# Counting the edge matrix of a graph network in steps of two edge tiles by 28 destinations

## The chip, the cores and the metric

The kernel runs on one core of one Trainium2 chip. The time is that of one execution on the device in microseconds; several runs were made, and their median counts.

## The reference

A graph of N = 6250 nodes with 128 features and E = 100000 edges. Edges are sorted by their destination `dst`, which is drawn as 6250 times the square of a uniform number, so low destinations have many more edges than high ones; `src` and the edge type (8 relations) are uniform. Two graph networks follow one another, each with a residual and a layer norm:

```python
def _rgcn_conv(x, src, dst, etype, bases_l, comp_l, root_l, bias_l):
    weight = jnp.einsum('rb,bio->rio', comp_l, bases_l)
    h = jnp.einsum('ni,rio->nro', x, weight)
    msg = h[src, etype]
    seg = dst * R + etype
    cnt = segment_sum(ones, seg, num_segments=N * R)
    norm = 1.0 / jnp.maximum(cnt[seg], 1.0)
    agg = segment_sum(msg * norm[:, None], dst, num_segments=N)
    return agg + x @ root_l + bias_l
# three such layers, batch norm and relu between them; then
#   x = layernorm(x + rgcn(x))
h = x @ W_in + b_in                         # 128 -> 64
deg = segment_sum(ones(E), src, N)
edge_weight = rsqrt(deg)[src] * rsqrt(deg)[dst]    # 0 where deg is 0
acc = cur = h
for _ in range(3):
    cur = segment_sum(cur[dst] * edge_weight[:, None], src, N)
    acc = acc + cur
x = layernorm(x + (acc / 4) @ W_out + b_out)
```

The three passes at the end multiply `cur` by one and the same matrix, whose element (src, dst) is the number of edges from src to dst. That matrix is what the change is about.

## The kernel before

Nodes are put into 49 blocks of 128 (NBLK = 49, NP = 6272), edges into 782 tiles of 128.

**Layers (window_sums).** For each tile, `one_sum` (lines 1046 to 1051) issues an indirect DMA on POOL that gathers 128 rows of `h_d` into a buffer `gt` (27 buffers), and a matmul on PE (L1051) sums them by destination with a one-hot `o`, which DVE makes for eight tiles at once (L1040, L1042). After each group of two tiles DVE adds the sum in PSUM to `agg` (L1630). Each layer gathers for 100 tiles of rows of x in `first_sums`, beside the matmuls that make h (L956), and for 590 tiles of rows of h in its window. The edges of the destinations with most edges are summed in another way, by `dense_sums`: seven chunks, each with a load of packed counts, preparation on DVE and ACT (L1326 to L1345) in single buffers, and 42 matmuls (L1352); its end are L1369 to L1383.

**Side work.** The layers' loop takes turns with other work, a generator `side_work`: first `hot_counts` (packed counts for dense_sums) and `degrees` (L1403 to L1415) in layer 0, then `counts`, which makes the edge matrix. `take_turns` spreads N_SIDE side turns over TURNS tiles. While dense_sums runs, its turns take the place of the side turns. The order in which the instructions stand on each engine is set when the program is built, and each engine works through its own in that order.

**The edge matrix.** Counts are packed into 32-bit words: a word has six fields (FLD = 6) of four bits, each for another block of src. There are NSL = 9 slices, so that one destination has S = 9 x 128 = 1152 words. `counts` goes through the edges in steps of TS = 4 tiles. A step adds to the words of one block of 128 destinations; a block whose edges reach over several steps is carried on, and there are NST = 245 steps. In each step:

- DVE makes `dst_hot` for four tiles (L1560, 128 x 512), the one-hot of the destination within the block.
- For each tile (a unit) DVE makes `row` (L1564): 1152 columns, in which one word holds 1 shifted to the field of this edge's src.
- PE multiplies dst_hot (weights, 128 columns) by row (moving, in pieces of 512, 512 and 128 columns) into three PSUM banks (L1577).
- `leave` adds each piece to what is carried, `had` times `keep` (L1535, three operations), and SP issues a DMA of `had` to `a_d` in DRAM (L1546), whose condition, read into registers for eight steps at a time, is true only where a block is done: 49 times of 245. The DMA writes 576 KB in pieces of 512 bytes.

Rows have four buffers (rp), had three (ac), dst_hot two (cp), and PSUM pool ps_w has five banks, which dense_sums takes all of.

**The tail.** Three passes, each over nine slices of src and seven chunks of seven blocks of destinations. SP loads a chunk `packed` (128 destinations by 7 x 128 words, 3584 bytes in a run; ten buffers), DVE splits it into two halves of fields (`u`, L1831 and L1832), and PE takes one field of one block at a time as weights and `three`, which holds cur in three bfloat16 parts and a one, as the moving side (L1837): 7203 matmuls.

Of the kernel before, what the change touches and what calls it, by code (L numbers as in the profile page):

```python
# [17 lines left out]
P = 128  # L18
# [501 lines left out]
def sorted_path(  # L520
# [34 lines left out]

    nc = tc.nc
# [48 lines left out]
    NG4 = Q * J // TS  # L605
    NST = NG4 + NBLK
# [6 lines left out]
    assert T1 + AND <= HT and P1 == 2 and W == 4 * P1 * P and 15 * NS1 <= NST * TS  # L613
    assert D == P and N * R <= 1 << 16 and R == 8 and H == 64
    assert 96 < Q <= P and N + P <= PAD and NBLK % CH == 0 and J == 2 * TS and NST <= 256
# [498 lines left out]
    ac = tc.alloc_tile_pool(name="ac", bufs=3)  # L1114
# [4 lines left out]
    a_d = dram.tile([NSL, P, NBLK, P], I32, name="a_d")  # L1119
    iota_c = kp.tile([P, S], mybir.dt.int16, name="iota_c")  # L1120
    nc.gpsimd.iota(iota_c, pattern=[[1, S]], base=0, channel_multiplier=0)
# [4 lines left out]
    nc.gpsimd.iota(iota_q, pattern=[[0, 1]], base=0, channel_multiplier=2,  # L1126
                   allow_small_or_imprecise_dtypes=True)

    e_src, e_rel, rel_s, e_val = (kp.tile([P, NST, TS], F32, name=f"e_tab{k}") for k in range(4))
# [10 lines left out]
    def hot_counts():  # L1140
# [130 lines left out]
        had = ac.tile([P, S], I32, name="had")  # L1271
        nc.vector.memset(had[:, :SR], 0)
        made, sums, at = {}, {}, {}
        for i in range(NS1 + 2):
            if i < NS1:
                hot = cp.tile([P, TS, P], BF16, name="dst_hot")
                nc.vector.tensor_tensor(hot[:, :P1, :], iota_f[:, None, :].to_broadcast([P, P1, P]),
                                        e_lo[:, i, :, None].to_broadcast([P, P1, P]), op=OP.is_equal)
                rows = []
                for j in range(P1):  # L1280
                    row = rp.tile([P, S], BF16, name="row")
                    nc.vector.tensor_scalar(row[:, :SR], iota_c[:, :SR], e_col[:, i, j : j + 1],
                                            e_v[:, i, j : j + 1], op0=OP.is_equal, op1=OP.mult)
                    rows.append(row)
                made[i] = hot, rows
            s = i - 1
            if 0 <= s < NS1:
                hot, rows = made.pop(s)
                sums[s] = ps_w.tile([P, 512], F32, name="pw")
                for j in range(P1):  # L1290
                    nc.tensor.matmul(sums[s][:, :SR], hot[:, j, :], rows[j][:, :SR], start=(j == 0),
                                     stop=(j == P1 - 1))
            s = i - 2
            if s >= 0:
                now = ac.tile([P, S], I32, name="had")
                nc.vector.scalar_tensor_tensor(now[:, :SR], had[:, :SR], keep[:, s : s + 1],
# [8 lines left out]
                nc.sync.dma_start(c1_d[:, bass.ds(at[0, s], 1), :], now[:, None, :SR], cond=(at[1, s] == 1))  # L1305
# [121 lines left out]
    def counts():  # L1427

        B = NBLK
        edge = kp.tile([P, B], F32, name="edge")  # L1430
        nc.vector.tensor_scalar(edge, iota_f[:, :B], float(P), None, op0=OP.mult)
        d_in = dst_f[:, 1 : W + 1]
        p_t = [ps_w.tile([P, 512], F32, name="pw")[:B, :1] for _ in range(2)]
        for h in range(2):
            below = [cp.tile([Q, B], F32, name=f"below{k}") for k in range(2)]
            nc.vector.tensor_scalar(below[0], edge[:Q, :], d_in[:, h * 512 + 511 : h * 512 + 512], None,
                                    op0=OP.is_gt)
            nc.vector.tensor_scalar(below[1], edge[:Q, :], float(P), d_in[:, h * 512 : h * 512 + 1],
                                    op0=OP.add, op1=OP.is_gt)
            for k in range(2):  # L1440
                nc.tensor.matmul(p_t[k], below[k], ones[:Q, :1], start=(h == 0), stop=(h == 1))
        col = kp.tile([B, 8], F32, name="col")
        t0, n, incl, s0, delta, pos, top = (col[:, i : i + 1] for i in range(7))
        nc.vector.tensor_copy(t0, p_t[0])
        nc.vector.tensor_tensor(n, p_t[1], t0, op=OP.subtract)
# [3 lines left out]
        p_i = ps_w.tile([P, 512], F32, name="pw")[:B, :1]  # L1449
        nc.tensor.matmul(p_i, upto, n, start=True, stop=True)  # L1450
        nc.vector.tensor_copy(incl, p_i)
        nc.vector.tensor_sub(s0, incl, n)
        nc.vector.tensor_sub(delta, t0, s0)
        nc.vector.tensor_scalar_add(top, incl, -1.0)
        yield

        fld = kp.tile([B, 2], F32, name="fld")
        nc.vector.tensor_scalar(fld[:, 0:1], iota_p[:B, :], float(NSL), None, op0=OP.is_ge)
        for j in range(2, FLD):
            nc.vector.scalar_tensor_tensor(fld[:, 0:1], iota_p[:B, :], float(j * NSL), fld[:, 0:1],  # L1460
                                           op0=OP.is_ge, op1=OP.add)
        nc.vector.scalar_tensor_tensor(fld[:, 1:2], fld[:, 0:1], -float(NSL), iota_p[:B, :],
                                       op0=OP.mult, op1=OP.add)
        FULL = NBLK - (FLD - 1) * NSL
        nc.vector.tensor_scalar(pos, fld[:, 1:2], -float(FULL), 0.0, op0=OP.add, op1=OP.max)
        nc.vector.tensor_sub(pos, fld[:, 0:1], pos)
        nc.vector.scalar_tensor_tensor(pos, fld[:, 1:2], float(FLD), pos, op0=OP.mult, op1=OP.add)

        past, within, start_, ends = (flat(e_val)[:B, i * NST : (i + 1) * NST] for i in range(4))
        nc.vector.tensor_scalar(past, iota_s[:B, :], incl, None, op0=OP.is_ge)  # L1470
        nc.vector.tensor_scalar(within, iota_s[:B, :], s0, None, op0=OP.is_ge)
        nc.vector.tensor_sub(within, within, past)
        nc.vector.tensor_scalar(start_, iota_s[:B, :], s0, None, op0=OP.is_equal)
        nc.vector.tensor_scalar(ends, iota_s[:B, :], top, None, op0=OP.is_equal)
# [3 lines left out]
        p_b = ps_w.tile([P, 512], F32, name="pw")  # L1478
        nc.tensor.matmul(p_b[:, :NST], ones[:B, :], past, start=True, stop=True)
        nc.vector.tensor_scalar(step_b, p_b[:, :NST], float(P), None, op0=OP.mult)  # L1480
        p_g = ps_w.tile([P, 512], F32, name="pw")
        delta_b = kp.tile([B, P], F32, name="delta_b")
        nc.vector.tensor_copy(delta_b, delta.to_broadcast([B, P]))
        nc.tensor.matmul(p_g[:, :NST], delta_b, within, start=True, stop=True)
        nc.vector.tensor_add(step_g, p_g[:, :NST], iota_s)
        p_k = ps_w.tile([P, 512], F32, name="pw")
        nc.tensor.matmul(p_k[:, :NST], ones[:B, :], start_, start=True, stop=True)
        nc.vector.tensor_scalar(keep, p_k[:, :NST], -1.0, 1.0, op0=OP.mult, op1=OP.add)
        step_i = kp.tile([1, 2, NST], I32, name="step_i")
        for k, of in enumerate((pos, ones[:B, :1])):  # L1490
            p_e = ps_w.tile([P, 512], F32, name="pw")
            nc.tensor.matmul(p_e[:1, :NST], of, ends, start=True, stop=True)
            nc.vector.tensor_copy(step_i[:, k, :], p_e[:1, :NST])
        yield

        sel = [flat(rel_s)[:Q, h * NST : (h + 1) * NST] for h in range(2)]
        for h in range(2):
# [3 lines left out]
        for to, of in ((e_key, key_f), (e_rel, d_in)):  # L1501
            for j in range(TS):
                pe = ps_w.tile([P, 512], F32, name="pw")
                for h in range(2):
                    c = h * 512 + j * P
                    nc.tensor.matmul(pe[:, :NST], of[:, c : c + P], sel[h], start=(h == 0), stop=(h == 1))
                nc.vector.tensor_copy(to[:, :, j], pe[:, :NST])
                yield
        nc.vector.tensor_scalar(e_key, e_key, 3, None, op0=OP.logical_shift_right)
        nc.vector.tensor_copy(e_src, e_key)  # L1510
        nc.vector.tensor_tensor(rel_s, e_rel, step_b[:, :, None].to_broadcast([P, NST, TS]),
                                op=OP.subtract)
        over = e_rel
        nc.vector.memset(e_val, 1.0)
        for j in range(1, FLD):
            nc.vector.tensor_scalar(over, e_src, float(j * S), 15.0, op0=OP.is_ge, op1=OP.mult)
            nc.vector.scalar_tensor_tensor(e_val, over, 1.0, e_val, op0=OP.add, op1=OP.mult)
        e_fld = over
        nc.vector.tensor_scalar(e_fld, e_src, float(S), None, op0=OP.is_ge)
        for j in range(2, FLD):  # L1520
            nc.vector.scalar_tensor_tensor(e_fld, e_src, float(j * S), e_fld, op0=OP.is_ge, op1=OP.add)
        nc.vector.scalar_tensor_tensor(e_src, e_fld, -float(S), e_src, op0=OP.mult, op1=OP.add)
        yield

        pieces = [(1024, S - 1024), (0, 512), (512, 512)]
        had = ac.tile([P, S], I32, name="had")
# [4 lines left out]
        def leave():  # L1531

            s, k, p, had, now = left.pop(0)
            c, w = pieces[k]
            nc.vector.scalar_tensor_tensor(now[:, c : c + w], had[:, c : c + w], keep[:, s : s + 1],  # L1535
# [386 lines left out]
```

## Time and profile before

| what | value |
|---|---|
| median of 3 runs | 3674.02 us (3672.62 to 3679.8) |
| profiled execution | 4294.16 us |
| its span | 4292.4 us |
| mean granted clock of TensorE | 0.72 |
| PE busy | 2957.9 us (69%) |
| DVE busy | 2451.4 us (57%) |
| POOL busy | 2114.4 us (49%) |

The profiled execution is 17% longer than the median of the runs; all durations from the trace belong to it. PE is the engine of matmuls, PEld its loading of weights (beside PE), DVE the vector engine, ACT the scalar one, POOL the one that issues the gathers, SP the one that issues the other DMAs. A line of a group of instructions gives: line, engine, operation, output <- inputs, partitions x elements and type of output and input, count | busy us, mean ns of one | idle time just before them, and what ended it. A line of waits gives the engine, what waits, what it waited for: us in total, number of times, longest us. "Issue" is time in which an engine waited for nothing that the profile shows, "remote" a wait whose end no engine of this core explains. A line of windows gives the stretch and its length in us, busy time (with the number of instructions) of PE, PEld, DVE, ACT and POOL, the granted clock, and the DMA engines' busy share and GB/s.

### The profile page before, as it was taken

Reading aid. Unit: us, or ns where it says so; the run is one execution under the profiler, and the core shown is the slowest. Engines: PE = TensorE matmul, PEld = TensorE weight load, DVE = VectorE, ACT = ScalarE, POOL = GpSimd, SP = SyncE. Lnnn points to the kernel's source line nnn. Section 1 sums busy time; section 2 is a strip of 40 time slices with the busy share of each in tenths; the row PEclk is TensorE's granted clock in tenths of the full one; section 3 lists DMA queues with packets and bytes.
Section 4 is the critical chain, followed back from the end, with each engine's and each line's share of the span. In section 5 each row is a group of like instructions: output and inputs, shape, how many; then the busy total and the mean of one; then the engine's idle time right before and its main releaser. Section 6 shows DMA issues by size and latency. Waiting matters only on the chain.

```text
span 4292.4 us, 51372 instructions
## 1 busy us (share of the span) xinstructions
PE 2957.9 (69%) x17520; PEld 2063.9 (48%) x17520; DVE 2451.4 (57%) x6315; ACT 322.6 (8%) x600; POOL 2114.4 (49%) x2083
## 2 busy tenths in 40 slices
PE   6745545667649576666666586766666756999998
PEld 3444434443334343334343334433333435999997
DVE  7557756752651376667526613766666435755555
ACT  2400000000005000000000041000000101000000
POOL 5566766564533665666664346655555653000000
PEclk8855555676669666667766687666666766999999
DMA  5511111131127111112231263222222312454542
GB/s 183 182 44 42 50 49 59 37 76 51 40 71 275 49 45 50 55 57 59 62 80 46 78 238 113 59 60 62 60 68 59 91 50 83 139 155 138 151 128 81
DMA packets 274421, 373.10 MB, mean 87 GB/s; under 512 B 86718, under 2 KB 197726, under 8 KB 274148
## 3 DMA queue, kind: packets, MB, share of 16 engines
q1 hardware_dynamic: 199464, 230.31, 16.9%
q0 software_dynamic: 66240, 135.79, 11.2%
q10 hardware_dynamic: 8444, 3.61, 0.3%
q8 instruction: 140, 2.29, 0.2%
q14 instruction: 133, 1.09, 0.1%
HBM read 250.74 MB, written 243.64 MB: 115 GB/s over the span
## 4 chain that ended last, share of the span: by engine, by line
PE 47%; DVE 25%; another core or an unknown queue 14%; issue 11%; DMA 1%; DVEq 1%; POOL 0%; ACTq 0%; ACT 0%; SPq 0%; POOLq 0%
PE pw L1837 13%; PE ps L1051 11%; PE pw L1577 8%; PE pw L956 6%; DVE row L1564 6%; DVE had L1535 5%; PE pw L1352 3%; DVE agg L1630 2%; DVE o L1040 2%; DVE dst_hot L1560 1%; DVE lo_hot L1403 1%; PE pw L1379 1%; PE pw L969 1%; DVE blk_hot L1406 1%
## 5 line engine op out<-in xcount | busy, mean ns | idle before, releaser
L1048 POOL DMA_INDIRECT gt<-h_d,gidx x1770 | 1796.1, 1015 | 1123.8 <-PE ps L1051 589.3
L1577 PE MATMUL pw<-row,dst_hot 128*128 128x128 bf16 (+1 forms) x2940 | 906.2, 439 | 645.2 <-issue 261.8
L1051 PEld LDWEIGHTS ps<-o,gt 128*128 128x128 f32 x4140 | 790.5, 273 | 366.3 <-issue 164.2
L1564 DVE TENSOR_SCALAR row<-iota_c,e_tab,e_tab 128x1152 bf16<-128x1152 int16 x980 | 566.1, 586 | 677.0 <-remote 385.2
L1051 PE MATMUL ps<-o,gt 128*128 128x48 f32 (+1 forms) x4140 | 785.5, 349 | 199.0 <-issue 71.2
L1577 PEld LDWEIGHTS <-dst_hot 128*128 128x128 bf16 x2940 | 353.2, 132 | 1075.0 <-issue 1011.7
L1837 PE MATMUL pw<-three,u 128*128 128x193 bf16 x7203 | 615.0, 248 | 13.8 <-DVE three L1764 10.1
L1837 PEld LDWEIGHTS <-u 128*128 128x128 fp8e3 x7203 | 601.7, 98 | 21.3 <-DVE three L1764 10.2
L1535 DVE SCALAR_TENSOR_TENSOR had<-had,keep,pw 128x128 int32<-128x128 int32 x735 | 444.8, 606 | 1.0 <-PE pw L1577 1.0
L956 PE MATMUL pw<-w,xT 128*128 128x512 f32 x588 | 295.0, 638 | 69.6 <-issue 40.0
L1048 POOL DMA_INDIRECT gt<-x_d,xidx x200 | 195.0, 975 | 268.4 <-PE ps L1051 122.7
L1831 DVE TENSOR_SCALAR u<-packed 128x896 int32<-128x896 int32 x189 | 117.8, 623 | 194.2 <-PE pw L1837 194.1
L1352 PE MATMUL pw<-x,u 128*128 128x385 bf16 x735 | 190.5, 388 | 49.4 <-issue 38.7
L1403 DVE TENSOR_TENSOR lo_hot<-iota_f,e_tab 128x512 bf16<-128x512 f32 x196 | 134.4, 686 | 140.7 <-remote 84.5
L956 PEld LDWEIGHTS pw<-w,xT 128*128 128x128 f32 x588 | 109.9, 202 | 174.0 <-issue 130.0
L1630 DVE TENSOR_TENSOR agg<-agg,ps 128x48 f32 x885 | 174.6, 197 | 31.6 <-PE ps L1051 20.3
L957 ACT COPY hs<-pw 128x512 f32<-128x512 f32 x294 | 171.1, 585 | 252.1 <-remote 119.1
L1415 PE MATMUL pd<-blk_hot,lo_hot 128*128 128x49 bf16 x782 | 62.8, 218 | 183.4 <-DVE blk_hot L1406 74.3
L1040 DVE TENSOR_TENSOR o<-iota_f,lo 128x384 f32<-128x384 f32 x222 | 121.9, 550 | 114.3 <-remote 70.3
L1352 PEld LDWEIGHTS <-u 128*128 128x128 fp8e3 x882 | 95.1, 112 | 157.5 <-issue 114.0
L1560 DVE TENSOR_TENSOR dst_hot<-iota_f,e_tab 128x512 bf16<-128x512 f32 x245 | 167.5, 684 | 0.0
L1415 PEld LDWEIGHTS <-lo_hot 128*128 128x128 bf16 x782 | 63.6, 130 | 207.1 <-DVE lo_hot L1403 132.7
(398 smaller groups left out, 1886.8 us busy)
## 6 DMA issues: line engine op xcount, KB each, us to landing
a_d<-had SPq DMA_DIRECT2D x245, 576.0 KB
packed<-a_d SPq DMA_DIRECT2D x189, 448.0 KB
h_d<-hs SPq DMA_DIRECT2D x147, 512.0 KB
gt<-h_d,gidx POOLq DMA_INDIRECT x1770
c_d<-had SPq DMA_DIRECT2D x62, 196.0 KB
packed<-c_d SPq DMA_DIRECT2D x21, 448.0 KB
x_d<-xc SPq DMA_DIRECT2D x24, 256.0 KB
xc<-in_x_dram SPq DMA_DIRECT2D x19, 256.0 KB
```

Of the source, the lines that this page charges most:

```text
L956: nc.tensor.matmul(ph, xT[:, b * P : (b + 1) * P], w[:, c : c + 512], start=True, stop=True)
L1040: nc.vector.tensor_tensor(o[:, :n, :width], iota_f[:, None, :width].to_broadcast([P, n, width]), column[:, t : t + n, None].to_broadcast([ ...
L1048: nc.gpsimd.indirect_dma_start(out=gt, out_offset=None, in_=table[:, :], in_offset=bass.IndirectOffsetOnAxis(ap=at[:, t : t + 1], axis=0))
L1051: nc.tensor.matmul(pa, gt, o, start=first_, stop=last)
L1352: nc.tensor.matmul(sums[d][:, :C3D], us[d % 2][:, i, :, d // 2], x3[:, i, :], start=(c == 0 and i == 0), stop=(c * CH + i == NBLK - 1))
L1403: nc.vector.tensor_tensor(hot[:, :n, :], iota_f[:, None, :].to_broadcast([P, n, P]), src_lo[:, t0 : t0 + n, None].to_broadcast([P, n, P]), ...
L1535: nc.vector.scalar_tensor_tensor(now[:, c : c + w], had[:, c : c + w], keep[:, s : s + 1], p[:, :w], op0=OP.mult, op1=OP.add)
L1560: nc.vector.tensor_tensor(hots[s], iota_f[:, None, :].to_broadcast([P, TS, P]), rel_s[:, s, :, None].to_broadcast([P, TS, P]), op=OP.is_equal)
L1564: nc.vector.tensor_scalar(rows[i], iota_c, e_src[:, s, j : j + 1], e_val[:, s, j : j + 1], op0=OP.is_equal, op1=OP.mult)
L1577: nc.tensor.matmul(p[:, :w], hots[s][:, j, :], row[:, c : c + w], start=(j == 0), stop=(j == TS - 1))
L1630: nc.vector.tensor_add(to, to, pa)
L1837: nc.tensor.matmul(out_of(f), bytes_[f % 2][:, d, :, f // 2], cur[:, order[c0 + d], :], start=(c0 + d == 0 and f % 2 == 0), stop=(c0 + d = ...
```

## The change

The matrix is counted and stored in another form.

- A step is two tiles (TU = 2) by 28 destinations (DB = 28); NP / DB = 224 blocks, NST = 616 steps. The number of units rises from 980 to 1232.
- The two sides of the count matmul are exchanged. `row` now has 252 columns, one for each of 28 destinations x 9, where the nine are what src / 128 leaves when the field is taken from it; its value is the field's shift, and its two halves of 126 columns (HB) are the weights. The one-hot is that of src's low seven bits (`dst_hot` by name still, made for four units at once) and is moving, 128 columns. A unit takes two matmuls rather than three, into one PSUM bank for each step.
- `had` is one operation of 126 x 256 for each step. The conditional DMA is issued for each of 616 steps, is true for 224, and writes 252 runs of 512 bytes.
- had has five buffers rather than three; iota_c, row and had are 392 elements wide rather than 1152.
- The tables that give each step its edges are made for two tiles a step, in four parts rather than two, and N_SIDE goes from 1263 to 1516 with TURNS unchanged.
- The matrix in DRAM is stored by destination: for each, nine runs of 128 words, one per slice of src. The tail reads a chunk of five or six blocks (each ninth) with runs of 512 bytes: 243 chunks rather than 189, with the same 7203 matmuls.

```diff
     TS = 4
-    NG4 = Q * J // TS
-    NST = NG4 + NBLK
+    TU = 2
+    DB = 28
+    NDB = NP // DB
+    HB = DB * NSL // 2
+    NST = Q * J // TU + NDB
...
-    ac = tc.alloc_tile_pool(name="ac", bufs=3)
+    ac = tc.alloc_tile_pool(name="ac", bufs=5)
...
-    a_d = dram.tile([NSL, P, NBLK, P], I32, name="a_d")
+    a_d = dram.tile([NDB, 2 * HB, P], I32, name="a_d")
...
-            s, k, p, had, now = left.pop(0)
-            c, w = pieces[k]
-            nc.vector.scalar_tensor_tensor(now[:, c : c + w], had[:, c : c + w], keep[:, s : s + 1],
-                                           p[:, :w], op0=OP.mult, op1=OP.add)
-            if k < len(pieces) - 1:
-                return
+            s, p, had, now = left.pop(0)
+            nc.vector.scalar_tensor_tensor(now[:HB, : 2 * P], had[:HB, : 2 * P], keep[:HB, s : s + 1],
+                                           p[:HB, : 2 * P], op0=OP.mult, op1=OP.add)
...
             nc.sync.dma_start(
-                a_d[:, :, bass.ds(at[0, s], 1), :].rearrange("s p d c -> p s (d c)"),
-                now.rearrange("p (s c) -> p s c", c=P), cond=(at[1, s] == 1))
+                a_d[bass.ds(at[0, s], 1), :, :].rearrange("k (c p) b -> p (k c) b", p=HB),
+                now[:HB, : 2 * P].rearrange("p (c b) -> p c b", c=2), cond=(at[1, s] == 1))
...
-        for i in range(NST * TS + LEAD):
-            s, j = divmod(i, TS)
+        for i in range(NST * TU + LEAD):
+            s, j = divmod(i, TU)
             if s < NST:
-                if j == 0:
-                    hots[s] = cp.tile([P, TS, P], BF16, name="dst_hot")
-                    nc.vector.tensor_tensor(hots[s], iota_f[:, None, :].to_broadcast([P, TS, P]),
-                                            rel_s[:, s, :, None].to_broadcast([P, TS, P]),
+                if i % TS == 0:
+                    hots[i // TS] = cp.tile([P, TS, P], BF16, name="dst_hot")
+                    nc.vector.tensor_tensor(hots[i // TS], iota_f[:, None, :].to_broadcast([P, TS, P]),
+                                            flat(e_lo)[:, i : i + TS, None].to_broadcast([P, TS, P]),
                                             op=OP.is_equal)
-                rows[i] = rp.tile([P, S], BF16, name="row")
-                nc.vector.tensor_scalar(rows[i], iota_c, e_src[:, s, j : j + 1], e_val[:, s, j : j + 1],
-                                        op0=OP.is_equal, op1=OP.mult)
+                rows[i] = rp.tile([P, SR], BF16, name="row")
+                nc.vector.tensor_scalar(rows[i][:, : 2 * HB], iota_c[:, : 2 * HB], e_col[:, s, j : j + 1],
+                                        e_val[:, s, j : j + 1], op0=OP.is_equal, op1=OP.mult)
...
-                sums[s] = [ps_w.tile([P, 512], F32, name="pw") for _ in pieces]
-            pa, row = sums[s], rows.pop(i - LEAD)
-            for (c, w), p in zip(pieces, pa):
-                nc.tensor.matmul(p[:, :w], hots[s][:, j, :], row[:, c : c + w], start=(j == 0),
-                                 stop=(j == TS - 1))
+                sums[s] = ps_w.tile([P, 512], F32, name="pw")
+            row = rows.pop(u)
+            for c in range(2):
+                nc.tensor.matmul(sums[s][:HB, c * P : (c + 1) * P], row[:, c * HB : (c + 1) * HB],
+                                 hots[u // TS][:, u % TS, :], start=(j == 0 and c == 0), stop=(j == TU - 1 and c == 1))
...
-    N_SIDE = 6 + NS1 + 2 + 2 + -(-NTS // TS) + 1 + 2 + 2 * TS + 1 + NST * TS + LEAD
+    N_SIDE = 6 + NS1 + 2 + 2 + -(-NTS // TS) + 1 + 5 + 2 * TU + 3 + NST * TU + LEAD
...
-            for c0 in range(0, NBLK, CH):
-                packed = ap_.tile([P, CH, P], I32, name="packed")
-                nc.sync.dma_start(packed, a_d[sl, :, c0 : c0 + CH, :])
+            for c0 in range(NSL):
+                blocks = list(range(c0, NBLK, NSL))
+                m = len(blocks)
+                packed = ap_.tile([P, FLD, P], I32, name="packed")
+                nc.sync.dma_start(packed[:, :m, :], a_rows[:, c0::NSL, sl, :])
```

## The prediction

> **What bounds the kernel now.** I read the busy line first, then the slices, then the chain that ended last.
>
> ```profile
> PE 2957.9 (69%) x17520; PEld 2063.9 (48%) x17520; DVE 2451.4 (57%) x6315; ACT 322.6 (8%) x600; POOL 2114.4 (49%) x2083
> PE 47%; DVE 25%; another core or an unknown queue 14%; issue 11%; DMA 1%; DVEq 1%; POOL 0%; ACTq 0%; ACT 0%; SPq 0%; POOLq 0%
> ```
>
> No engine is full over the span, so the stages have different limits. The slices show two regimes: up to 3600 us the gathers run on POOL beside everything else; after that POOL is idle and PE is full. The three layers' windows (590 gathers each) run from 207 to 1239, 1424 to 2435 and 2622 to 3589 us: 1032, 1011 and 967 us.
>
> The groups give the prices, the waits say who holds whom.
>
> ```profile
> L1048 POOL DMA_INDIRECT gt<-h_d,gidx x1770 | 1796.1, 1015 | 1123.8 <-PE ps L1051 589.3
> L1577 PE MATMUL pw<-row,dst_hot 128*128 128x128 bf16 (+1 forms) x2940 | 906.2, 439 | 645.2 <-issue 261.8
> L1564 DVE TENSOR_SCALAR row<-iota_c,e_tab,e_tab 128x1152 bf16<-128x1152 int16 x980 | 566.1, 586 | 677.0 <-remote 385.2
> L1560 DVE TENSOR_TENSOR dst_hot<-iota_f,e_tab 128x512 bf16<-128x512 f32 x245 | 167.5, 684 | 0.0
> L1837 PE MATMUL pw<-three,u 128*128 128x193 bf16 x7203 | 615.0, 248 | 13.8 <-DVE three L1764 10.1
> ...
> POOL gt L1048 <- PE ps L1051: 762.8, 374, 40.3
> POOL gt L1048 <- issue: 395.1, 1264, 1.7
> DVE row L1564 <- remote: 385.2, 66, 26.1
> PE pw L1577 <- DVE had L1535: 246.3, 147, 20.5
> ```
>
> A gather costs POOL 1.015 us and an "issue" gap of 395.1/1264 = 0.31 us: 1.325 us, unless it waits for PE to free one of 27 gt buffers, which it does for 762.8 us. So POOL may run 27 x 1.25 = 34 us ahead of PE (1.25 us is the period of gathers in an unbroken streak), and then stops. Where counting stands beside gathers (1959 us, 1194 gathers, 980 rows) one gather takes 1.64 us: 1.325 is POOL's own, the rest is PE, late with counts and rows. The row waits called "remote" (up to 26.1 us) fall into streaks in which POOL issues gather after gather while PE has long finished; had (one input in PSUM) never shows them.
>
> One stage shows what a gather costs when counting is thin: the dense sums, with 34 to 36 gathers in 50 us (1.39 to 1.47 us each) though PE is busy for 38 of them.
>
> ```profile
> 950.00:1000.00 50.00, 38.13 (x170) 22.73 (x168) 14.39 (x38) 4.45 (x8) 33.39 (x34) 0.66 0.32 81
> 2150.00:2200.00 50.00, 37.69 (x221) 26.18 (x219) 16.51 (x45) 6.20 (x11) 35.12 (x36) 0.81 0.41 102
> 3600.00:4292.00 692.00, 662.93 (x7501) 643.43 (x7501) 421.71 (x1265) 51.58 (x139) 0.16 (x1) 0.97 0.43 132
> ```
>
> The last line is the tail: PE 96% busy at a clock of 0.97, so PE sets it.
>
> **What the Trainium skill says.** "SBUF — State Buffer", section "Who interferes with whom": a DVE operation with two SBUF inputs or in a two-port mode contends with GpSimd for one port pair, and the second to issue is fully blocked. The trace agrees for row, o and lo_hot (385, 147 and 84 us of "remote") and for the absence of such waits at had and agg. "TensorE: Matmul & The Clock Gate", section "Weight-path perf modes": fast weight load asks for 128 columns that aren't fp32; the new count weights have 126. No row of before shows 126. "DMA: Bandwidth & Descriptors", section "Specifications": 512 B is the smallest transfer at line rate. The trace agrees loosely: packets of 512 B took 27 ns (median), of 3584 B 187 ns (mean), 19 B per ns either way.
>
> **The change, part by part.**
>
> *DVE.* Start to start, a row of 1152 takes 0.49 us, had 0.66 + 0.66 + 0.26 us for four units, dst_hot 0.60 us for four: 0.49 + 0.395 + 0.15 = 1.035 us per unit, 980 units, 1014 us. After: a row of 252, for which the row of 392 (382 ns recorded) and of 1152 (586) give about 330 ns recorded, 0.26 us start to start; had of 256 lies between 338 (128 wide) and 740 (512), 0.39 us for two units; dst_hot unchanged. 0.26 + 0.195 + 0.15 = 0.605 us, 1232 units, 745 us: DVE is relieved of some 270 us. But there are 1232 rows and 308 hots instead of 980 and 245 that can be blocked by gathers.
>
> *PE.* Ten count matmuls took 3.6 to 3.8 us at half clock, 1.15 us per unit, 1130 us in all. Two matmuls of 128 columns at 0.11 (the L1837 matmuls run at 0.085) to 0.21 us each (estimate; the upper one at half clock) are 0.22 to 0.43 us per unit, 270 to 530 us: 600 to 850 us less. If all this were on the path, the layers would fall to POOL's floor.
>
> *Where the work stands.* The instruction order of the two built programs decides how much of it counts. Before, about 126 count matmuls stand among each 50 gather matmuls on PE, and the dense matmuls come in 42s with 16 gathers between. After, layers 1 and 2 have only some 44 count matmuls (22 units, 11 steps) per 50 gathers. Then, with no gather matmul among them, come 340 count matmuls, 287 dense ones and the dense end in layer 1, and a like block in layer 2; in layer 0, 280 dense ones with 16 gathers among them. In both programs steps go by at about 11 per 50 gathers; a step now holds half the units. Each a_d issue is chained to the one before, and there are 616 instead of 245, which fits.
>
> *Cost of the block.* 170 units at DVE's 0.605 us are 103 us. SP may be slower: it takes 0.5 to 0.7 us for a false step and about 2.2 us for eight steps' registers; a true write of 576 KB held it for 3.7 us, one of 126 KB I put at 2 to 2.7 us (estimate). With 45% true that is about 1.6 us per step, 136 us for 85 steps. I take 120. Dense: 42 matmuls took 8.8 us (2184.1 to 2192.9), and about 3.3 us of u, xc and x work precede them in single buffers: 7 x 12 = 84 us. Its end takes some 20 us. Sum 224 us, of which POOL covers 34: 190 us of standstill for the gathers, in layer 1 and again in layer 2. In layer 0: 84 + 20 - 34 = 70 us.
>
> *The gathers between.* The floor is 1.325 us; the dense stage, with PE nearly full, gave 1.39 at best; degrees (300 to 750 us) about 1.57. I take 1.38, with 1.33 and 1.45 as ends. Layer 1: 590 x 1.38 = 814, + 190, + 46 for the layer's change = 1050 us against 1011: +39. Layer 2: 814 + 190 = 1004 against 967: +37. Layer 0: 275 gathers beside degrees at 1.6 = 440, 315 x 1.38 = 435, + 70 + 46 = 991 against 1032: -41.
>
> *Setup of counts.* More marks, transposed tables of 616 steps, 16 quarter sums: some 40 extra operations of 0.3 us on DVE, +10 us, partly covered by gathers.
>
> *Tail.* 7203 matmuls as before; 243 reads of up to 384 KB in runs of 512 B for 189 in runs of 3584 B. Per engine: before 24192 x 187 ns / 16 = 283 us, after 165375 x 27 to 29 ns / 16 = 279 to 300 us, within 640 us of PE and ten tiles ahead. PE hides it up to 62 ns per packet. u has 486 operations of 768 for 378 of 896: +30 us on DVE, 61% busy there. Taken as 0, ends -10 and +20.
>
> *Sum.* +39 + 37 - 41 + 10 = +45 us on 4294.16 us (span 4292.4): 4339. The median of the runs, 3674.02, is 0.856 of the profiled execution; 4339 x 0.8556 = **3712 us**.
>
> **The rivals.**
>
> *POOL at its floor* (32%). With DVE and PE this light, nothing but a gather's 1.325 us counts between the blocks, and the counting block takes 85 us: standstill 85 + 84 + 20 - 34 = 155. Layer 1: 782 + 155 + 46 = 983 (-28), layer 2: 937 (-30), layer 0: 440 + 417 + 70 + 46 = 973 (-59), setup +10: -107, 4187, scaled 3582 us: **faster**. For it: 1264 of the gathers had no wait but the gap. Against: degrees, at half of PE, still gave 1.57. It decides from about 1.35 us per gather with 190 us of standstill.
>
> *No standstill* (5%). The blocks cost nothing beyond the floor: 828, 782 and 903 us, -497 + 10, 3807, scaled 3257 us. Against: on an in-order PE a gather matmul behind 600 others cannot free its buffer.
>
> *SP paces the block* (9%). If each step waits 2.7 us for its write, true or not, 85 steps take 230 us: 110 us more in each of two layers, 265 in all, 4559, scaled 3901 us. Against: SP's wait for a_d was 74 us in all, 24 times.
>
> *The change doesn't do what it says*: the counts of instructions and shapes in the built program agree with it, so I give this nothing.
>
> **How the numbers follow.** The likeliest case has 54%; its own range, from 1.33 and 1.45 us per gather and a standstill of 160 to 220 us, is 3620 to 3810. What a measurement can tell from no change is about 0.2%. Of the 54, 44 lie over it, 5 within, 5 below. Faster: 5 + 32 + 5 = 42%; same 5%; slower 44 + 9 = 53%. The range 3560 to 3860 leaves out no standstill (5), most of SP's case (7) and the end of the floor case (6).
>
> **What would show it.** Right: in each of layers 1 and 2 a stretch of 150 to 220 us without gathers, in which PE shows only counts and then dense sums; "POOL waits for PE" with longest waits of over 100 us; 1.33 to 1.45 us per gather elsewhere; row near 330 ns and had near 470; the tail at 690 us. Wrong: gathers that run through the blocks; 1.5 us and more between them (PE then waits for rows blocked by gathers); a tail over 720 us (reads or u); SP waits on a_d of more than 300 us.

## The result, and the profile after

| | median | range | runs |
|---|---|---|---|
| kernel before | 3673.32 us | 3670.88 to 3679.8 | 4 |
| changed kernel | 4084.51 us | 4079.08 to 4088.2 | 4 |

The ratio is 1.1115, 95% interval [1.1094, 1.1136]: 11% slower. 3712 us had been forecast, with a range to 3860. The profiled execution of the changed kernel took 4079.08 us (span 4077.2), no longer than its other runs, while that of before had taken 4294.16 against 3674. That is the first thing to explain. In one set of runs below, on a chip of its own, the kernel before takes some 4280 us, as in the profile before (here called the long condition), and in the others, on two further chips, some 3670 us, as in the runs (the short condition).

The waits of the changed kernel (whole span; engine, what waits, for what: total us, times, longest):

```profile
DVE row L1576 <- PE pw L1590: 804.9, 357, 11.9
POOL gt L1053 <- PE ps L1056: 630.8, 300, 218.4
PE pw L1590 <- DVE had L1549: 456.9, 337, 3.0
POOL gt L1053 <- issue: 191.8, 629, 0.3
SPq L1558 <- DMA a_d<-had: 283.3, 192, 3.3
```

No line here is "remote": of the 385 us for row before, nothing is left. POOL waits for PE for 631 us in sum, where it had waited for 763, but once for 218 us, where 40 was the longest. The timeline of POOL shows that gap in layer 1 (start, us, ...; in brackets the idle time before):

```profile
1931.35 0.95 POOL L1053 DMA_INDIRECT gt<-h_d,gidx  x1 [0.31 <-PE pw L1590]
1932.60 0.95 POOL L1053 DMA_INDIRECT gt<-h_d,gidx  x1 [0.30 <-issue]
2151.97 0.98 POOL L1053 DMA_INDIRECT gt<-h_d,gidx  x1 [218.42 <-PE ps L1056]
```

A second one, 211.1 us from start to start, lies in layer 2 (3085.2 to 3296.3), and one of 60.5 in layer 0 (941.4 to 1001.9). Everywhere else the gathers of layers 1 and 2 are 1.28 us apart on average. What PE does meanwhile, by its timeline and the windows (us, PE, PEld, DVE, ACT, POOL busy, clock, DMA share, GB/s):

```profile
1980.90 0.69 PE L1590 MATMUL pw<-dst_hot,row 128*126 128x128 bf16 x4 [1.47 <-DVE had L1549]
1982.45 0.69 PE L1590 MATMUL pw<-dst_hot,row 128*126 128x128 bf16 x4 [0.87 <-DVE had L1549]
1984.62 0.69 PE L1590 MATMUL pw<-dst_hot,row 128*126 128x128 bf16 x4 [1.47 <-DVE had L1549]
```

```profile
1900.00:2060.00 160.00, 59.28 (x344) 43.18 (x344) 110.20 (x298) 0.00 (x0) 25.62 (x27) 0.50 0.14 39
2060.00:2138.00 78.00, 65.93 (x314) 33.96 (x315) 30.92 (x69) 13.43 (x24) 0.00 (x0) 0.90 0.30 69
3390.00:4077.00 687.00, 657.88 (x7488) 638.31 (x7486) 436.01 (x1358) 51.46 (x139) 0.00 (x0) 0.98 0.46 131
```

From 1900 to 2060 us PE makes the block of counts, one step of four matmuls every 1.56 or 2.16 us (1.86 on average), and waits for had each time; POOL gets off 27 more gathers and then stands. From 2060 to 2138 come the dense sums, with POOL at 0. After that PE waits 12 us more for a row. The last line is the tail.

The groups that answer to those shown of before (by form):

```profile
L1053 POOL DMA_INDIRECT gt<-h_d,gidx x1770 | 1801.2, 1018 | 1030.2 <-PE ps L1056 557.6 <-DMA gt<-h_d,gidx 262.2 <-issue 156.4
L1854 PE MATMUL pw<-three,u 128*128 128x193 bf16 x7203 | 616.7, 248 | 14.8 <-issue 9.9 <-ACT three L1776 2.6 <-DVE sums L1873 1.4
L1590 PE MATMUL pw<-dst_hot,row 128*126 128x128 bf16 x2464 | 410.2, 322 | 523.5 <-DVE had L1549 456.9 <-DVE row L1576 63.5 <-DVE xc L1707 2.5
L1576 DVE TENSOR_SCALAR row<-iota_c,e_tab,e_tab 128x252 bf16<-128x252 int16 x1232 | 383.0, 355 | 806.6 <-PE pw L1590 804.9 <-PE ps L1056 0.2
L1549 DVE SCALAR_TENSOR_TENSOR had<-had,keep,pw 126x256 int32<-126x256 int32 x616 | 291.7, 473 | 0.3
L1572 DVE TENSOR_TENSOR dst_hot<-iota_f,e_tab 128x512 bf16<-128x512 f32 x308 | 210.6, 684 | 0.0
```

The group of had in the kernel before:

```profile
L1535 DVE SCALAR_TENSOR_TENSOR had<-had,keep,pw 128x128 int32<-128x128 int32 x735 | 444.8, 606 | 1.0 <-PE pw L1577 1.0
```

The operations are as cheap as hoped: row, had and dst_hot together took 566.1 + 444.8 + 167.5 = 1178 us before and take 383.0 + 291.7 + 210.6 = 885 now, and the count matmuls 410 us rather than 906. The time is lost all the same.

### The profile page after: what moved, and what is told of

It reads as the page before. It is cut to its first block, busy times and chain, and to the rows that moved or that the text cites. A ratio compares the mean times of both kernels' runs of the same rounds, so it can differ in the third digit from the quotient of the medians.

```text
span 4077.2 us, 53463 instructions
## 1 busy us (share of the span) xinstructions
PE 2755.0 (68%) x17110; PEld 2199.1 (54%) x17110; DVE 2223.1 (55%) x6623; ACT 323.7 (8%) x600; POOL 2118.8 (52%) x2083
## 4 chain that ended last, share of the span: by engine, by line
PE 41%; DMA 26%; DVE 22%; issue 6%; POOL 3%; DVEq 0%; ACT 0%; POOLq 0%; SPq 0%; ACTq 0%
DMA gt<-h_d,gidx 25%; PE pw L1854 14%; PE ps L1056 9%; PE pw L961 6%; DVE row L1576 5%; PE pw L1590 4%; DVE had L1549 3%; POOL gt L1053 3%; PE pw L1357 3%; DVE dst_hot L1572 2%; DVE agg L1644 1%; DVE o L1045 1%; DVE lo_hot L1408 1%; PE pw L1384 1%; DVE o L1047 1%
## 5 line engine op out<-in xcount | busy, mean ns | idle before, releaser
L1056 PE MATMUL ps<-o,gt 128*128 128x48 f32 (+1 forms) x4140 | 1075.3, 401 | 536.5 <-DMA gt<-h_d,gidx 439.4
L1056 PEld LDWEIGHTS ps<-o,gt 128*128 128x128 f32 x4140 | 939.0, 307 | 753.8 <-DMA gt<-h_d,gidx 562.0
L1576 DVE TENSOR_SCALAR row<-iota_c,e_tab,e_tab 128x252 bf16<-128x252 int16 x1232 | 383.0, 355 | 806.6 <-PE pw L1590 804.9
L1590 PE MATMUL pw<-dst_hot,row 128*126 128x128 bf16 x2464 | 410.2, 322 | 523.5 <-DVE had L1549 456.9
L1590 PEld LDWEIGHTS <-row 128*126 128x126 bf16 x2464 | 314.7, 217 | 606.0 <-DVE had L1549 520.8
L1549 DVE SCALAR_TENSOR_TENSOR had<-had,keep,pw 126x256 int32<-126x256 int32 x616 | 291.7, 473 | 0.3
L1848 DVE TENSOR_SCALAR u<-packed 128x640 int32<-128x640 int32 (+1 forms) x243 | 126.5, 521 | 203.2 <-PE pw L1854 201.1
L1572 DVE TENSOR_TENSOR dst_hot<-iota_f,e_tab 128x512 bf16<-128x512 f32 x308 | 210.6, 684 | 0.0
L1357 PE MATMUL pw<-x,u 128*128 128x385 bf16 x735 | 158.5, 355 | 27.8 <-DVE x L1350 16.4
L1053 POOL DMA_INDIRECT gt<-in_x_dram,xidx x100 | 121.0, 1210 | 71.8 <-PE ps L1056 41.4
```

The lines of the kernel that those rows point to most:

```text
L1053: nc.gpsimd.indirect_dma_start(out=gt, out_offset=None, in_=table[:, :], in_offset=bass.IndirectOffsetOnAxis(ap=at[:, t : t + 1], axis=0))
L1056: nc.tensor.matmul(pa, gt, o, start=first_, stop=last)
L1357: nc.tensor.matmul(sums[d][:, :C3D], us[d % 2][:, i, :, d // 2], x3[:, i, :], start=(c == 0 and i == 0), stop=(c * CH + i == NBLK - 1))
L1549: nc.vector.scalar_tensor_tensor(now[:HB, : 2 * P], had[:HB, : 2 * P], keep[:HB, s : s + 1], p[:HB, : 2 * P], op0=OP.mult, op1=OP.add)
L1572: nc.vector.tensor_tensor(hots[i // TS], iota_f[:, None, :].to_broadcast([P, TS, P]), flat(e_lo)[:, i : i + TS, None].to_broadcast([P, TS, ...
L1576: nc.vector.tensor_scalar(rows[i][:, : 2 * HB], iota_c[:, : 2 * HB], e_col[:, s, j : j + 1], e_val[:, s, j : j + 1], op0=OP.is_equal, op1= ...
```

## The experiments

**The kernel before, profiled again, twice.** No edit.

> The kernel before, unchanged, profiled again. Theory A (the profiled execution of before was longer than its ordinary ones by foreign waits): the row, o and lo_hot waits called remote, some 620 us in the first profile, are nearly gone (under 60 us), and the span is 3640 to 3700 us, near the runs' median. Theory B (what was seen belongs to the kernel under the profiler): span 4250 to 4330 us again, with 550 to 680 us of remote waits.

> The kernel before, unchanged, for a profile of the condition of this comparison. If its time is near 3674 us, the remote waits on row, o and lo_hot are under 60 us in all, and the gathers of a window stand 1.25 to 1.35 us apart; if near 4274, they are over 500 us again.

The first of these two executions met the long condition: 4281.0 us, span 4279.2, with these waits:

```profile
DVE row L1564 <- remote: 393.5, 64, 26.1
DVE o L1040 <- remote: 143.3, 15, 24.0
DVE lo_hot L1403 <- remote: 93.7, 13, 13.5
ACT hs L957 <- remote: 73.5, 3, 62.9
POOL gt L1048 <- remote: 67.7, 92, 3.7
```

These are the numbers of theory B, but its reason, the profiler, falls: the seven runs of before beside it took 4273.65 us in the median, and the second execution, profiled as well but on another chip, took 3677.97 us, span 3676.1, with no remote wait on any engine:

```profile
DVE row L1564 <- PE pw L1577: 295.7, 155, 10.4
POOL gt L1048 <- PE ps L1051: 222.1, 400, 13.2
POOL gt L1048 <- DMA gt<-h_d,gidx: 213.3, 700, 0.3
```

The spans differ by 4279.2 - 3676.1 = 603 us. The sums of the waits can't be set against that one by one, since not every wait holds up the end. The chain that ended last can (first e1, then e6; "another core or an unknown queue" is its name for remote waits):

```profile
PE 45%; DVE 26%; another core or an unknown queue 15%; issue 11%; DMA 1%; DVEq 1%; ACT 0%; POOL 0%; ACTq 0%; POOLq 0%; SPq 0%
PE 52%; DVE 26%; DMA 12%; issue 8%; POOL 2%; DVEq 1%; ACT 0%; POOLq 0%; SPq 0%; ACTq 0%
```

These waits have 15% of 4279 us, some 640 us, in the long condition, and do not appear in the short one. The program is the same. The profile from which was forecast shows the long condition, its runs the short one. And in the short one, POOL waits for PE for only 222 us, never over 13.2 at a time: the gathers of before stand 1.31 to 1.32 us apart in layers 1 and 2, the one stop of 11 us at the dense sums left out. The unbroken streak has 1.25 and the changed kernel reaches 1.28, so less work on DVE and PE has little left to gain in these windows.

The kept trace also says what "remote" stands for here. By its record of the semaphores, the counters by which engines tell each other that work is done, each of the 212 remote waits of e1, on whatever engine, ended with an update of PE's semaphore, and this update came 4.7 us in the median, and up to 22.6 us, after the last recorded end of a PE instruction that makes such updates. In the short condition (e6) 1586 waits ended with an update of this semaphore, and none came over 0.02 us after such an end. So the engines waited for word from PE, and it came late; whether PE's work or only its signal was late, the traces don't tell. One such wait of e1, by the timeline; PE's last work before it ends at 1466.3:

```profile
1462.58 3.72 PE L1577 MATMUL pw<-row,dst_hot 128*128 128x512 bf16 x10
1485.60 0.58 DVE L1564 TENSOR_SCALAR row<-iota_c,e_tab,e_tab 128x1152 bf16<-128x1152 int16 x1 [24.93 <-remote]
```

**The changed kernel, again.** No edit.

> The changed kernel, unchanged, beside the kernel before. Two conditions have been seen: before at 3674 us, and before at 4274 us with 600 us of remote waits on DVE (e1). Theory A (the forecast failed because the profile of before was of the second condition and the times of the first; the changed kernel loses in both by its blocks): where before takes about 4270 us, the changed kernel takes 4330 to 4480 us, with remote waits of over 300 us and gaps of about 200 us between gathers in layers 1 and 2; where before takes about 3674, it takes 4060 to 4100 with no remote waits. Theory B (the changed kernel is immune to the remote waits): 4060 to 4120 us in both.

> The changed kernel, unchanged. Where the kernel before takes about 3672 us: 4070 to 4100. Where it takes about 4274 (the condition with remote waits): 4330 to 4480, with remote waits over 300 us.

4083.27 us beside 3671.38 (ratio 1.1116 [1.1089, 1.1143]), and 4089.27 beside 3670.9 (1.1127 [1.1107, 1.1147]), with no remote waits. Both met the short condition, where both theories say the same; what they say of the long one was not tried.

The stages, from the first gather of each on POOL's timeline, of three kernels run side by side in the short condition:

| stage | before (e6) | changed (e5) | coarse (e7) |
|---|---|---|---|
| up to the first window | 196.9 | 195.0 | 196.1 |
| layer 0, window | 874.2 | 939.6 | 876.9 |
| layer 1, first sums | 148.9 | 132.6 | 136.8 |
| layer 1, window | 833.0 | 1016.6 | 817.4 |
| layer 2, first sums | 153.0 | 138.1 | 136.9 |
| layer 2, window | 773.3 | 962.2 | 771.8 |
| after it (tail) | 696.7 | 704.1 | 698.3 |
| span | 3676.1 | 4088.3 | 3634.1 |

Of +412 us, the three windows make 65 + 184 + 189 = 438; first sums give back 31; the tail costs 7.

**Fewer, larger steps: "coarse".** The same form with half the issues of `a_d`, which form a chain, since each waits for the one before:

```diff
-    TU = 2
-    DB = 28
-    HB = DB * NSL // 2
+    TU = 4
+    DB = 56
+    NQ = 4
+    HB = DB * NSL // NQ
...
-            for c in range(2):
+            for c in range(NQ):
                 nc.tensor.matmul(sums[s][:HB, c * P : (c + 1) * P], row[:, c * HB : (c + 1) * HB],
```

> The changed kernel's form, but in steps of four tiles by 56 destinations: 308 steps and a_d issues in one chain in place of 616, with four halves of 126 columns per unit, rows of 504 and had of 126 x 512. No block of counts stands ahead of the dense sums. Theory of the chain (the number of chained a_d issues sets how the counts are laid out at build time, and the block is the loss): the two gaps of 219 and 211 us between gathers and the one of 60 us vanish, 3560 to 3680 us, about as before or a little faster. Rival (the exchanged form itself is slow: weights of 126 columns, rows, the tail's short runs): 4000 to 4150 us, no better than the changed kernel.

> As e2_coarse (steps of four tiles by 56 destinations, 308 chained issues, no block). Where before takes about 3674 us, theory of the chain: 3520 to 3680 us, no remote waits. Rival (the exchanged form loses by itself): 3750 us and more. Where before takes about 4270: 4150 to 4210 as in e2.

In the long condition 4166.8 us beside 4273.65 (0.9763 [0.9688, 0.9839]); in the short one 3637.2 beside 3671.38 (0.9904 [0.9873, 0.9936]). This is the exchanged form, with 126 columns of weights, 1232 units and the tail's short runs, and it is a little ahead of before in both, by 2.4% and 1.0%: the form as such loses nothing. The windows of e7 have no gap over 13 us outside the change of layers, and POOL waits for PE no longer than in before:

```profile
POOL gt L1056 <- DMA gt<-h_d,gidx: 236.1, 775, 0.3
POOL gt L1056 <- PE ps L1059: 162.2, 300, 11.8
```

By the table the gain, 42 us, comes from the first sums (28 us) and layer 1's window (16); the windows of layers 0 and 2 do not move. The 4167 us of the long condition, above my 3560 to 3680, are to be read beside the 4274 of before there. In that condition the windows took 1018.2, 975.7 and 937.3 us (e2), those of before 1018.8, 1033.6 and 948.7 (e1): 70 us less in all. The remote waits did not shrink with the work there, and PE had some too (e2):

```profile
DVE row L1579 <- remote: 509.1, 129, 11.4
PE pw L1593 <- remote: 149.9, 30, 10.5
```

**The chain of issues alone.** Coarse, and the kernel before, with each a_d DMA issued twice, same data, same place:

```diff
-            nc.sync.dma_start(a_d[...], now[...], cond=(at[1, s] == 1))
+            for _ in range(2):
+                nc.sync.dma_start(a_d[...], now[...], cond=(at[1, s] == 1))
```

> As e2_coarse, but each conditional a_d DMA is issued twice (the same data to the same place): 616 chained issues as in the changed kernel, nothing else added. Blocks of 613 and 736 count matmuls (some 150 and 180 units) then stand ahead of the dense sums of layers 1 and 2. Theory of the chain: gaps of 200 to 300 us between gathers come back in both layers, 4000 to 4250 us. Rival (the issues cost nothing where they don't wait): within 40 us of e2_coarse.

> Steps of four tiles by 56 destinations with every a_d issue doubled (616 chained issues), as e3. Where the kernel before takes about 3672 us: coarse without the doubling took 3637; theory of the chain: 4020 to 4160, with two gaps of 200 to 260 us between gathers. Rival (the block costs much only together with remote waits): under 3850.

> The kernel before, with each conditional a_d DMA issued twice: 490 chained issues in place of 245, the form of the count unchanged. Blocks of 356 and 532 count matmuls (119 and 177 units) stand ahead of the dense sums. Theory of the chain: it becomes slow like the changed kernel, 3900 to 4100 us. Rival (only the new form is slow): 3670 to 3750 us, the second writes being hidden.

> The kernel before with every a_d issue doubled (490 chained issues), as e4. Where the kernel before takes about 3672 us: theory of the chain: 3950 to 4120, with two gaps of 190 to 270 us between gathers. Rival: under 3850.

| | issues in the chain | long condition | short condition | gaps in layers 1 and 2 (short) |
|---|---|---|---|---|
| before | 245 | 4273.65 | 3671.38 | none over 20 us |
| before, twice | 490 | 4633.97 | 4059.14 | 171.3 and 219.8 |
| coarse | 308 | 4166.8 | 3637.2 | none over 20 us |
| coarse, twice | 616 | 4635.55 | 4073.69 | 202.7 and 220.0 |
| changed | 616 | not measured | 4083.27 | 219.2 and 211.3 |

("Gaps" are stretches between the starts of two gathers, the change of layers left out. The doubled kernels of the short condition ran in another set than the rest of their column; before took 3670.9 us there.) POOL's timeline at the end of the gap in layer 1, first of before and then of coarse, each with doubled issues:

```profile
2079.69 1.46 POOL L1048 DMA_INDIRECT gt<-h_d,gidx  x1 [170.36 <-PE ps L1051]
```

```profile
2138.81 0.94 POOL L1056 DMA_INDIRECT gt<-h_d,gidx  x1 [201.80 <-PE ps L1059]
```

Doubling the issues costs coarse 436 us and the old form 388, and gives both gaps like the changed kernel's. The ratios to before in the short condition are 1.1088 [1.1069, 1.1107] and 1.105 [1.1025, 1.1075], the changed kernel's own within 1%. In the order of the built instructions, both doubled programs have blocks of 356 to 736 count matmuls ahead of the dense sums of layers 1 and 2, the changed kernel of 340 and more. The traces show the same on PE: from one gather matmul to the next, in layers 1 and 2, stand 613 and 736 count matmuls (coarse, twice, e3), 356 and 532 (before, twice, e4), 352 and 356 (changed), and nowhere over 66 in before and coarse. So the number of these issues is what sets the block, and the block is the loss. That it acts through their waiting for one another was not tried by itself (as many issues without a chain), nor how the build makes blocks of it. In the long condition, where I had expected 3900 to 4250 us, the doubled ones took 4634 and 4636: 360 and 469 us more than their own bases, about the same step.

**More row buffers.** In the block DVE's rows wait for PE to free a buffer, and had stands behind them. Six row buffers rather than four (and four of had rather than five):

```diff
-    rp = tc.alloc_tile_pool(name="rp", bufs=4)
-    ac = tc.alloc_tile_pool(name="ac", bufs=5)
+    rp = tc.alloc_tile_pool(name="rp", bufs=6)
+    ac = tc.alloc_tile_pool(name="ac", bufs=4)
```

> The changed kernel with six row buffers in place of four (and four of had in place of five, for the space). The block of counts is as long (360 and 366 count matmuls), but its rows no longer have to wait in DVE's queue, ahead of had, for PE to free a buffer. Theory (the pace of the block, 1.86 us per step, is the circle of PE, row buffer, row and had): the pace falls to DVE's own 1.2 to 1.35 us per step, the gaps between gathers fall from 219 and 211 to 160 to 180 us, and the time is 60 to 110 us below the changed kernel's. Rival (one PSUM bank or SP's chain of writes sets the pace): 1.7 us per step or more, within 30 us of the changed kernel.

4114.27 us, 25 more than the changed kernel beside it (4089.27), with gaps of 223.1 and 214.3 us. The theory fell; within the block, 1935 to 2060 us, this kernel waits as the changed one does:

```profile
PE pw L1590 <- DVE had L1549: 79.0, 67, 1.5
DVE row L1576 <- PE pw L1590: 38.0, 67, 0.6
SPq L1558 <- DVE had L1549: 47.2, 42, 1.7
SPq L1558 <- DMA a_d<-had: 25.2, 18, 1.7
```

67 steps in 125 us are 1.87 us each. PE waits for had once per step although ps_w has five banks. The likely reason is that the dense sums, which take all five, already hold four while the block runs, so that a step's bank is free only after the had of the step before; this was argued from the waits and not tried. SP is not the pace: of these 125 us it waited 47 for had and only 25 for earlier writes.

**Rows made earlier.** Coarse with LEAD 5 rather than 3, six row buffers, three of dst_hot, four of had.

> As e7_coarse_again, with rows made five units ahead of their matmul rather than three (six row buffers, three of dst_hot, four of had). If PE's waits for rows and had pace the gathers, 20 to 80 us less than e7; if POOL's own rate of 1.25 us paces them, within 15 us of e7.

3667.71 us (0.9987 [0.9977, 0.9998]), 30 us above e7, neither of the two. The windows of layers 1 and 2 are as in e7 (818.4 and 769.9 us), so earlier rows gain nothing there; layer 0's is 918.0 rather than 876.9. What costs 41 us there is open.

## Why the prediction was wrong

It was right in direction and in what causes the loss, and wrong in size by a factor of about eleven: +38 us, 1%, was forecast, and +411, 11%, measured. The direction was in part luck: in its sum a loss of 450 us stood against a gain of 415.

- **The step that failed is the gain that was set against the standstill:** "1.325 is POOL's own, the rest is PE, late with counts and rows", so that lighter counts would bring a gather from 1.64 us to 1.38. In the sum of the forecast, the windows without their standstills fall from 1032 + 1011 + 967 = 3010 us to 921 + 860 + 814 = 2595: a gain of 415 us, which all but cancels the 450 of standstill.

  There was no such gain. In the condition of the runs the gathers of before stand 1.31 to 1.32 us apart in layers 1 and 2 (e6), 0.03 to 0.04 above the changed kernel's; coarse, which is nearly as light and has no block, gains 14 us in the three windows. Even in the long condition, where the 1.64 us come from, coarse gains 70. The 1.64 was due to the remote waits, which the same program does not have in the short condition, and not to the amount of counting. The forecast had named the 1232 rows "that can be blocked by gathers" and put this at nothing; those waits on row went from 393.5 us (e1) to 509.1 (e2). Without the gain, the forecast's own standstill of 190 + 190 + 70 us on the span of 3676 gives 4126, and 4088 was measured.
- **The last line of the sum, the factor 0.856, is the same error once more.** It took the 620 us between the profiled execution and the runs for a stretch of every stage. They were remote waits beside gathers, which the runs did not have. The profile had shown them (14.4% of the chain, 618 us), and 4294 - 618 = 3676 is the time of the runs. The factor alone moved little, +45 us to +38; but to ask where the 620 us lay would have shown that the 1.64 us was not the runs' own.
- **The gathers between** were put at 1.38 us (1.33 to 1.45); 1.28 was measured. The value came from the dense stage, which had remote waits as well. The floor of 1.325 was too high too: its gaps "issue" of 0.31 us are right, but a gather in a streak is 0.94 us long and not 1.015, which is the mean over all.
- **The standstill** was the best part: 190, 190 and 70 us forecast, 219, 211 and 60.5 measured. That the sums came out so near is in part luck, for the errors of the parts partly cancel. The counting block of layer 1 was 158 us (85 steps at 1.86) for 120: DVE's sum of 1.21 us per step is right as work, but PE and DVE took turns rather than overlapped. Dense and its end were 78 us for 104, and 12 us for the first row after them had been left out.
- **The prices** of single operations held: row 355 ns for 330, had 473 for about 470, four count matmuls (two units) 0.69 us for 0.44 to 0.86. The relief of DVE, 1178 - 885 = 293 us busy, was forecast as 270. The weights of 126 columns took 217 ns to load, those of 128 had taken 132 (at a mean granted clock of 0.66 and 0.72); coarse has loads of 126 columns as well (213 ns) and loses nothing.
- **The tail** was right: 696.7 before, 704.1 after in one set of runs, PE 96% busy as before (657.88 of 687 us); reads in runs of 512 bytes are hidden. Two slips in its working change nothing: the chunks have 27 x 49 x 128 = 169344 runs rather than 165375, and "19 B per ns either way" sets a median beside a mean.
- **The rivals.** "POOL at its floor" came nearest to the rate of gathers, with the wrong consequence, since before was nearly at that floor already. "No standstill" fell with the gap of 218 us. "SP paces the block" was not seen: the waits for a_d were 283 us over the whole kernel, near the 300 that had been named as the sign, but 3.3 at the longest, and within the block SP waits longer for had than for its writes. The range, up to 3860, had no case in which the runs lack the remote waits.
- **The port pair.** The Trainium skill's "SBUF — State Buffer", section "Who interferes with whom", was taken as the reason for the remote waits, and the trace was said to agree. The trace does not bear it out: ACT and POOL have such waits too (119.1 us on hs and 64.9 on gt in the profile before), PE in e2, and all end with a late update of PE's semaphore. (For an operation with two SBUF inputs the section asks besides that the GpSimd instruction reads SBUF; that was not shown for the gathers.) In the short condition the same operations run beside gathers without any. What differs between the conditions was not found; each chip was met once, so the chip itself and the moment can't be told apart.

## What to carry to other kernels

Where the profiled execution is longer than the runs, find which waits make the difference, subtract those, and only then ask what a stage has left to gain; a common factor is right only if every stage is stretched alike. When the order of instructions is fixed at build time, count the issues before counting the work: halving the tiles of a step and raising the number of issues from 245 to 616 turned work that lay beside the gathers into blocks that stand in front of them. With steps of four tiles by 56 destinations, the same form takes 1% less than before.

## What the runs showed of the hardware that was not expected

One and the same program took 4273.65 us in the median on one chip and 3671.38 on another, with a spread of under 1% on each. In the traces the difference lies in waits called remote, on DVE above all but on ACT, POOL and PE too, only while gathers were issued; the tail was the same (700 and 697 us). Each of these waits ended with an update of PE's semaphore that came up to 22.6 us after the last recorded end on PE (e1), where in the short condition it came within 0.02 us (e6). Why is open. The doubled issues cost about as much in both conditions (360 and 388 us in the old form), so these differences between kernels kept their sign.
